# Layer 3's last element: the final check in the written order behind the last centring, the mean behind the variance, the last normalisation in whole passes

## The chip, the cores and the metric

The kernel runs on one core of a Trainium2 chip. The metric is the device time of one execution in microseconds (us). Before the change it is 1911.26 us, the median of four runs (1908.66 to 1915.75).

## The reference

Sixteen graphs of 1024 nodes with 64 features pass through four layers. Each layer computes something on the graph, adds its input, and normalises every row of 64 to mean 0 and variance 1. The last layer, which the change touches, is an attention with four heads, followed by a second attention over the same adjacency, a leaky ReLU, a normalisation with gamma and beta, and then the residual and the layer's own normalisation:

```python
out_h = _gat_layer(h, mask[None, None], bh[None, :, None, :])
cat = jnp.transpose(out_h, (0, 2, 1, 3)).reshape(B, N, H * D)
z = jax.nn.leaky_relu(cat, negative_slope=0.2)
h2 = jnp.einsum('bnk,dk->bnd', z, Wo)
out2 = _gat_layer(h2, mask[None], bo)
z2 = jax.nn.leaky_relu(out2, negative_slope=0.2)
mu = jnp.mean(z2, axis=-1, keepdims=True)
var = jnp.mean(jnp.square(z2 - mu), axis=-1, keepdims=True)
out = (z2 - mu) * jax.lax.rsqrt(var + LN_EPS) * gamma + beta
...
x = _layernorm(x + out, axis=-1)
```

## The kernel before

Nodes lie on the 128 partitions, eight to each, so that a graph is a tile of 128 x 8 x 64 (a "128x512" instruction goes over a whole graph, a "128x64" one over one eighth of it). The layers run one after the other, and in each the 16 graphs. In layer 3 the work of a graph `b` is cut into bursts; lists named `mids` and `slots` give, by graph and burst, the smaller tasks that go between the attention's units, and `run(plan)` and `run(last)` (L2229) issue all of it. Both stand in a `manual_schedule` for the five engines (L2264): inside it each engine keeps the order in which the program issues its instructions. What stands outside is placed by the scheduler of the framework where it finds room, and it may put it between instructions of the written order.

The last graph, `E` = 15, has nothing behind it that could hide its end. Its tasks at the last burst are, in order (L2149): two of the checks, the second normalisation of graph 14 up to its power (`residual_power`), the sums of the last attention (`add_all`), `last_layer`, `shifted` and later `rows_2` of graph 14, `last_quotient`, and `last_norms` (L1733).

`last_norms` normalises twice. Each time `statistics` (L1717) calls `bn_stats` on VectorE (DVE) for the eight slices of 64, which gives count, mean and squared deviations of even and odd elements. From these it forms on VectorE, in tiles of 128x8, the difference `d` of the two means (L1724), the sum of deviations `var` (L1725), `mean` (L1726), the square of `d` in place (L1727), `var` over 64 plus epsilon (L1728) and the final variance (L1729). GpSimd (POOL) raises it to the power of -0.5 (L1730). The first time, eight instructions over one slice each subtract the mean and multiply with gamma (L1737), and eight more multiply with `rstd`, the power, and add the residual (L1739); beta was added to the residual long before (L2156). The second time, one pass subtracts the mean (L1743, the centring), and two halves are multiplied with `rstd` and stored on the queue of Sync (SP), each as soon as it is there (L1748, L1749).

The kernel is a fast path which is exact only if certain values stay in bounds. `check` (L2246) compares such values with a bound and writes the smallest result into a column of `flags`. The last check, of the attention sums of graph 15, stands behind the written order (L2272): a comparison and a reduction (L2248, L2249), the smallest over all flags (L2274), a transposition by TensorE (PE) so that the 128 partitions come into one row (L2276), the smallest of that row (L2278), and the flag `redo` (L2279). At the kernel's very end every engine loads `redo` into a register (`values_load`, L2289) and branches (L2290): where it is 1, a general path computes everything anew; with these inputs it is 0, and the branch skips it. Sync also asserts that the register lies between 0 and 1. Behind the branch Sync waits for the stores and the engines, and a closing round of drains and semaphores ends the program.

Of the kernel before, what the change touches and what calls it, by code (L numbers as in the profile page):

```python
# [8 lines left out]
F32 = mybir.dt.float32  # L9
# [4 lines left out]
ALU = mybir.AluOpType  # L14
AX = mybir.AxisListType

P = 128
FLT_MAX = 3.4028234e38
LN_EPS = 1e-5
# [8 lines left out]
LEAST_SUM = 1e-25  # L28
# [554 lines left out]
def fast_path(  # L583
# [24 lines left out]
    nc = tc.nc  # L608
    B, N, D = x.shape
    C = N // P  # L610
    H = L3_Wh.shape[0]
# [20 lines left out]
    small = ctx.enter_context(tc.tile_pool(name="small", bufs=4))  # L632
# [11 lines left out]
    def xb(b):  # L644
        return xg[b // GB][:, :, b % GB, :]
# [10 lines left out]
    ident = const.tile([P, P], F32, tag="ident", name="ident")  # L656
# [5 lines left out]
    neg_half = const.tile([P, C], F32, tag="neg_half", name="neg_half")  # L662
# [30 lines left out]
    def two_banks(name):  # L693

        if "s" in rings:
            t = rings["s"].tile([P, 2, HALF], F32, tag="s", name=name)
            return [t[:, i, :] for i in range(2)]
        return [ps_t.tile([P, HALF], F32, tag="t", name=name) for _ in range(2)]

    def one_bank(name):  # L700
        if "s" in rings:
            return two_banks(name)[0]
        return ps_t.tile([P, HALF], F32, tag="t", name=name)

    def bc_last(ap, n):

        return ap.unsqueeze(2).to_broadcast([P, ap.shape[1], n])

    def bc_mid(ap, n):

        return ap.unsqueeze(1).to_broadcast([P, n, ap.shape[1]])
# [614 lines left out]
    sums = const.tile([P, B, H + 1, C], F32, tag="sums", name="sums")  # L1326

    bo, gamma, beta = (const.tile([P, D], F32, tag=k, name=k) for k in ("bo", "gamma", "beta"))
# [294 lines left out]
    def head_out(b):  # L1623
# [93 lines left out]
        def statistics(src):  # L1717
            st = small.tile([P, C, 6], F32, tag="bn2", name="bn2", bufs=2)
            for c in range(C):
                nc.vector.bn_stats(st[:, c, :], src[:, c, :])  # L1720
            d, var, mean, rstd = (
                small.tile([P, C], F32, tag=f"last_{k}", name=f"last_{k}", bufs=2) for k in ("d", "var", "mean", "rstd")
            )
            nc.vector.tensor_tensor(d, st[:, :, 1], st[:, :, 4], ALU.subtract)  # L1724
            nc.vector.tensor_tensor(var, st[:, :, 2], st[:, :, 5], ALU.add)  # L1725
            nc.vector.scalar_tensor_tensor(mean, d, 0.5, st[:, :, 4], ALU.mult, ALU.add)  # L1726
            nc.vector.scalar_tensor_tensor(d, d, 0.25, d, ALU.mult, ALU.mult)  # L1727
            nc.vector.tensor_scalar(var, var, 1.0 / D, LN_EPS, ALU.mult, ALU.add)  # L1728
            nc.vector.tensor_tensor(var, var, d, ALU.add)  # L1729
            nc.gpsimd.tensor_tensor(rstd, var, neg_half, ALU.pow)  # L1730
            return mean, rstd

        def last_norms():  # L1733
            v, m = held["v"], held["m"]
            mean, rstd = statistics(v)
            for c in range(C):
                nc.vector.scalar_tensor_tensor(m[:, c, :], v[:, c, :], mean[:, c : c + 1], gamma, ALU.subtract, ALU.mult)  # L1737
            for c in range(C):
                nc.vector.scalar_tensor_tensor(  # L1739
                    v[:, c, :], m[:, c, :], rstd[:, c : c + 1], xb(b)[:, c, :], ALU.mult, ALU.add  # L1740
                )
            mean, rstd = statistics(v)
            nc.vector.tensor_tensor(m, v, bc_last(mean, D), ALU.subtract)  # L1743
            res = ep.tile([P, C, D], F32, tag="m", name="res", bufs=4)
            o = out[b].rearrange("(p c) d -> p c d", c=C)
            for h in range(2):
                part = slice(h * CH, (h + 1) * CH)
                nc.vector.tensor_tensor(res[:, part], m[:, part], bc_last(rstd[:, part], D), ALU.mult)  # L1748
                nc.sync.dma_start(o[:, part], res[:, part])  # L1749
# [61 lines left out]
        def residual_power():  # L1811
            residual_sum()
            held["n2"] = statistics(held["m"])
# [129 lines left out]
    with tc.tile_pool(name="ps_g", bufs=1, space=bass.MemoryType.PSUM, reuse_waits="tile") as ps_g, tc.tile_pool(  # L1943
        name="ps_u", bufs=2, space=bass.MemoryType.PSUM, reuse_waits="tile"
# [167 lines left out]
    E = B - 1  # L2112
# [69 lines left out]
    with tc.tile_pool(name="ps_g", bufs=1, space=bass.MemoryType.PSUM, reuse_waits="tile") as ps_g, tc.tile_pool(  # L2182
        name="ps_p", bufs=1, space=bass.MemoryType.PSUM, reuse_waits="tile"
# [32 lines left out]
    for b in range(B):  # L2216
        units = work[b][0][0] + work[b][1][0]
        outer = outs[b - 1][1][0] if b else []
        for j in range(BURSTS):
            n = (2, 2, 3, 5)[j - 4] if b >= E - 1 and j >= 4 else 5 if j < 4 else 3  # L2220
            burst, units = units[:n], units[n:]
            m = 5 - n
# [6 lines left out]
    def run(plan):  # L2229
        for b, j, burst in plan:  # L2230
            catch_up()
            made = [(unit, unit[0]()) for unit in burst]
            tasks(mids, b, j)
            while roots:
                roots.pop(0)()
            drain()
            made = [(product, mask(e)) for (_, mask, product), e in made]
            waiting.extend(lambda product=product, e=e: product(e) for product, e in made)
            if (b, j, burst) == plan[-1]:
                drain()  # L2240
            tasks(slots, b, j)

    flags = small.tile([P, 11], F32, tag="flags", name="flags", bufs=1)
    nc.vector.memset(flags, 1.0)

    def check(i, ap, op, bound):  # L2246
        t = small.tile([P, B * (H + 1) * C], F32, tag="ok", name="ok", bufs=1)[:, : ap.shape[1]]
        nc.vector.tensor_scalar(t, ap, bound, None, op)  # L2248
        nc.vector.tensor_reduce(flags[:, i : i + 1], t, AX.X, ALU.min)  # L2249

    known = []
# [8 lines left out]
    def look(some):  # L2260
        for one in some:
            check(known.index(one), *one)

    with tc.manual_schedule(engines=in_order | {mybir.EngineType.SP}):  # L2264
        run(plan)
        run(last)

    check(len(known), sums[:, E, H, :], ALU.is_ge, LEAST_SUM)  # L2272
    least = small.tile([P, 1], F32, tag="least", name="least")
    nc.vector.tensor_reduce(least, flags, AX.X, ALU.min)  # L2274
    pl = one_bank("pl")
    nc.tensor.transpose(pl[:1, :P], least, ident)  # L2276
    least1 = small.tile([1, 1], F32, tag="least1", name="least1")
    nc.vector.tensor_reduce(least1, pl[:1, :P], AX.X, ALU.min)  # L2278
    nc.vector.tensor_scalar(redo, least1, -1.0, 1.0, ALU.mult, ALU.add)  # L2279


def kernel(tc, *args):


    nc = tc.nc
    with tc.tile_pool(name="flag", bufs=1) as fp:
        redo = fp.tile([1, 1], I32, tag="redo", name="redo")
        fast_path(tc, redo, *args)
        again = nc.values_load(redo[0:1, 0:1], min_val=0, max_val=1)  # L2289
        with tc.If(again == 1):  # L2290
            general_path(tc, *args)
# [32 lines left out]
```

## Time and profile before

| what | value |
|---|---|
| median of four runs | 1911.26 us |
| the profiled execution | 1917.18 us, of which the span is 1915.4 us |
| mean granted TensorE clock | 0.987 |
| TensorE busy | 1863.6 us (97%) |
| VectorE busy | 1746.7 us (91%) |
| ScalarE busy | 1322.7 us (69%) |
| GpSimd busy | 102.0 us (5%) |
| VectorE busy, 1904.00 to 1907.70 | 3.60 of 3.70 us |
| VectorE busy, 1907.70 to 1910.00 | 0.77 of 2.30 us |
| GpSimd busy, 1907.70 to 1910.00 | 1.93 us |

The page gives busy time by engine over the whole span, in which the last fifteen microseconds count for less than one per cent. They are read from the timeline (one row for an instruction or a run of like ones, with its start from the beginning of the span, its time, line, operation, output and inputs, and in brackets the idle time of its engine before it and what ended it) and from the view of one line, which also has what a sequencer does by itself: loads of registers, branches and waits. These are not counted as busy time. Durations of neighbours can overlap: an instruction may start before the one ahead of it has ended, if it doesn't read its result.

### The profile page before, as it was taken

What the parts mean: (1) busy time and instruction counts of PE and PEld (TensorE: products, weight loads), DVE (VectorE), ACT (ScalarE), POOL (GpSimd) and SP (SyncE); (2) the same over time, 40 slices, a digit from 0 to 9 for tenths busy, and PEclk for the clock granted to TensorE, in tenths of its full rate; (3) what the DMA queues carried; (4) which work ended last, traced back from release to release, by engine and by line L of the source; (5) the groups of instructions that cost most, each with busy time, mean ns of one, the idle gap of its engine ahead of it and who ended that gap; (6) DMA issues with size and microseconds to landing.
All of it is one profiled execution on the core that took longest, in us unless ns stands there. A gap on an engine that the chain in (4) does not pass through costs nothing. (4 is left out here: it accounts for less than half of the span.)

```text
span 1915.4 us, 25738 instructions
## 1 busy us (share of the span) xinstructions
PE 1863.6 (97%) x9505; PEld 768.0 (40%) x9505; DVE 1746.7 (91%) x2913; ACT 1322.7 (69%) x2336; POOL 102.0 (5%) x93
## 2 busy tenths in 40 slices
PE   8999989999999999999999999999999999999996
PEld 4344337874433333333333333333333333333332
DVE  6899998899999988899998998999989899899996
ACT  3556567867888677676777667767667766776754
POOL 0000000001121000000000000000000000000001
PEclk8999989999999999999999999999999999999998
DMA  7000000002232300000010000100001000010000
GB/s 184 1 1 1 1 1 1 1 1 17 23 26 25 89 12 19 17 12 18 12 29 18 12 18 12 27 20 12 18 13 29 18 12 18 13 29 18 12 23 13
DMA packets 60308, 39.56 MB, mean 21 GB/s; under 512 B 51855, under 2 KB 52176, under 8 KB 60174
## 3 DMA queue, kind: packets, MB, share of 16 engines
q1 hardware_dynamic: 43534, 33.64, 6.7%
q0 software_dynamic: 14560, 3.67, 2.5%
q8 instruction: 76, 1.25, 0.3%
q10 hardware_dynamic: 2080, 0.52, 0.1%
q14 instruction: 58, 0.48, 0.1%
HBM read 29.45 MB, written 4.70 MB: 18 GB/s over the span
## 5 line engine op out<-in xcount | busy, mean ns | idle before, releaser
L1469 ACT ACTIVATE e<-s,shift 128x1024 f32<-128x1024 f32 x512 | 539.1, 1123 | 239.4 <-PE s L1465 239.4
L1473 DVE TENSOR_TENSOR e<-e,aT 128x1024 f32<-128x1024 f32 x512 | 597.8, 1218 | 3.1 <-ACT e L1469 2.9
L1465 PE MATMUL s<-hT 64*128 64x512 f32 x2048 | 489.1, 602 | 1.6 <-ACT zT L1512 1.2
L1480 PE MATMUL y<-e,vals 128*64 128x512 f32 x2048 | 483.4, 599 | 1.8 <-DVE e L1473 0.9
L1465 PEld LDWEIGHTS s<-hT 64*128 64x128 f32 x2048 | 183.9, 185 | 286.7 <-issue 143.5
L1480 PEld LDWEIGHTS y<-e,vals 128*64 128x64 f32 x2048 | 135.2, 136 | 269.0 <-issue 197.5
L1053 DVE SCALAR_TENSOR_TENSOR e<-G_l,q,aT 128x1024 f32<-128x1024 f32 x150 | 185.9, 1276 | 1.2 <-ACT G_l L1012 0.6
L1649 DVE TENSOR_TENSOR e<-e,aT 128x1024 f32<-128x1024 f32 x128 | 156.4, 1225 | 13.1 <-ACT e L1636 3.1
L1065 PE MATMUL y_l<-e,vals_l 128*64 128x512 f32 x608 | 146.2, 608 | 2.5 <-DVE e L1053 2.3
L1641 DVE SCALAR_TENSOR_TENSOR junk<-e,aN 128x1024 bf16<-128x1024 f32 x120 | 146.0, 1217 | 0.0
L1636 ACT ACTIVATE e<-s,shift 128x1024 f32<-128x1024 f32 x128 | 138.7, 1114 | 4.0 <-PE s L1631 3.9
L1631 PE MATMUL s<-h2T 64*128 64x512 f32 x512 | 127.5, 598 | 0.0
L1657 PE MATMUL y<-e,h2v 128*64 128x512 f32 x512 | 125.6, 592 | 0.0
L1408 POOL PARTITION_ALL_REDUCE gtop<-top x48 | 54.6, 1137 | 1214.7 <-DVE top L1406 1047.1
L2031 PE MATMUL po<-hi,aR 128*128 128x512 f32 x256 | 102.9, 403 | 10.9 <-ACT hi L1935 7.1
L2031 PE MATMUL po<-lo,aR 128*128 128x512 f32 x256 | 101.1, 396 | 0.3 <-DVE lo L1936 0.3
L793 ACT ACTIVATE x<-m,bn_shift,bn_rstd 128x64 f32<-128x64 f32 x216 | 74.6, 429 | 18.5 <-DVE bn_shift L784 18.5
L1631 PEld LDWEIGHTS s<-h2T 64*128 64x128 f32 x512 | 51.8, 189 | 60.1 <-issue 37.6
L1512 ACT COPY zT<-poT 64x512 f32<-64x512 f32 x124 | 72.0, 581 | 1.1
L1065 PEld LDWEIGHTS y_l<-e,vals_l 128*64 128x64 f32 x608 | 38.4, 136 | 76.0 <-issue 61.0
L1487 ACT COPY yT<-y 128x512 f32<-128x512 f32 x64 | 38.5, 601 | 43.5 <-PE y L1480 42.2
L1657 PEld LDWEIGHTS y<-e,h2v 128*64 128x64 f32 x512 | 36.6, 137 | 73.5 <-issue 59.5
(305 smaller groups left out, 2163.1 us busy)
## 6 DMA issues: line engine op xcount, KB each, us to landing
r<-inverse SPq DMA_DIRECT2D x62, 256.0 KB
adj<-in_adj_dram SPq DMA_DIRECT2D x16, 512.0 KB
out_dram<-res SPq DMA_DIRECT2D x15, 256.0 KB
x<-in_x_dram SPq DMA_DIRECT2D x14, 256.0 KB
m<-x POOLq DMA_DIRECT2D x14, 256.0 KB, 5.1
rows<-yT SPq DMA_DIRECT2D x62, 4.0 KB
x<-in_x_dram ACTq DMA_DIRECT2D x2, 256.0 KB
sums<-rows SPq DMA_DIRECT2D x31, 8.0 KB
```

Source lines behind the costliest of these rows:

```text
L1053: nc.vector.scalar_tensor_tensor(e, of_pair(b - b % 2, b % 2), pq[b - b % 2][1][:, k, b % 2 : b % 2 + 1], aT[:, k, :], ALU.max, ALU.mult,)
L1065: nc.tensor.matmul(held["y"][h * D : (h + 1) * D, :], vals[b][:, k, :], e[:, h * HALF : (h + 1) * HALF], start=(k == 0), stop=(k == C - 1),)
L1465: nc.tensor.matmul(s[:, i, :], hT[rows, k * P : (k + 1) * P], hT[rows, cols], start=True, stop=True)
L1469: nc.scalar.activation(e, s, AF.Exp, bias=shifts[b, n])
L1473: nc.vector.tensor_tensor(e, e, bc_mid(aT[:, k, h * HALF : (h + 1) * HALF], 2), ALU.mult)
L1480: nc.tensor.matmul(held[h][i * D : (i + 1) * D, :], vals[b][:, k, :], e[:, i, :], start=(k == 0), stop=(k == C - 1),)
L1631: nc.tensor.matmul(s[:, i, :], hT[rows, (i + k // CH) % 2, k % CH * P : (k % CH + 1) * P], hT[rows, 0, :], start=True, stop=True,)
L1636: nc.scalar.activation(e, s, AF.Exp, bias=shifts[b])
L1641: nc.vector.scalar_tensor_tensor(junk.rearrange("p c q -> p (c q)").bitcast(BF16), e.rearrange("p i q -> p (i q)"), 1.0, aN[:, k, :], ALU. ...
L1649: nc.vector.tensor_tensor(e, e, aT[:, k, :].rearrange("p (i q) -> p i q", i=2), ALU.mult)
L1657: nc.tensor.matmul(held["o"][h * D : (h + 1) * D, :], vals["out", b][:, k, :], e[:, h, :], start=(k == 0), stop=(k == C - 1),)
L2031: nc.tensor.matmul(po.rearrange("p q k f -> p (q k f)"), aR[:, k, ic * P : (ic + 1) * P], e[:, k].rearrange("p q k f -> p (q k f)"), start ...
```

## The change

Three things. In `statistics`, the mean goes behind the power, and the square of `d` gets a tile of its own (`last_square`), since `mean` still reads `d`. In `last_norms`, the first normalisation is four passes over the whole tile (subtract the mean, times gamma, times the power, plus the residual) where it was sixteen instructions over slices. And the last check moves, unchanged in itself, from behind the written order into it: `last_check` is called between the centring and the product with the last power. `statistics` also serves graph 14 (`residual_power`), so that the new order holds there too.

```diff
             nc.vector.tensor_tensor(d, st[:, :, 1], st[:, :, 4], ALU.subtract)
             nc.vector.tensor_tensor(var, st[:, :, 2], st[:, :, 5], ALU.add)
+            nc.vector.tensor_scalar(var, var, 1.0 / D, LN_EPS, ALU.mult, ALU.add)
+            square = small.tile([P, C], F32, tag="last_square", name="last_square", bufs=2)
+            nc.vector.scalar_tensor_tensor(square, d, 0.25, d, ALU.mult, ALU.mult)
+            nc.vector.tensor_tensor(var, var, square, ALU.add)
+            nc.gpsimd.tensor_tensor(rstd, var, neg_half, ALU.pow)
             nc.vector.scalar_tensor_tensor(mean, d, 0.5, st[:, :, 4], ALU.mult, ALU.add)
-            nc.vector.scalar_tensor_tensor(d, d, 0.25, d, ALU.mult, ALU.mult)
-            nc.vector.tensor_scalar(var, var, 1.0 / D, LN_EPS, ALU.mult, ALU.add)
-            nc.vector.tensor_tensor(var, var, d, ALU.add)
-            nc.gpsimd.tensor_tensor(rstd, var, neg_half, ALU.pow)
             return mean, rstd
...
         def last_norms():
             v, m = held["v"], held["m"]
             mean, rstd = statistics(v)
-            for c in range(C):
-                nc.vector.scalar_tensor_tensor(m[:, c, :], v[:, c, :], mean[:, c : c + 1], gamma, ALU.subtract, ALU.mult)
-            for c in range(C):
-                nc.vector.scalar_tensor_tensor(
-                    v[:, c, :], m[:, c, :], rstd[:, c : c + 1], xb(b)[:, c, :], ALU.mult, ALU.add
-                )
+            nc.vector.tensor_tensor(m, v, bc_last(mean, D), ALU.subtract)
+            nc.vector.tensor_tensor(m, m, bc_mid(gamma, C), ALU.mult)
+            nc.vector.tensor_tensor(m, m, bc_last(rstd, D), ALU.mult)
+            nc.vector.tensor_tensor(v, m, xb(b), ALU.add)
             mean, rstd = statistics(v)
             nc.vector.tensor_tensor(m, v, bc_last(mean, D), ALU.subtract)
+            last_check()
             res = ep.tile([P, C, D], F32, tag="m", name="res", bufs=4)
...
+    def last_check():
+        check(len(known), sums[:, E, H, :], ALU.is_ge, LEAST_SUM)
+        least = small.tile([P, 1], F32, tag="least", name="least")
+        nc.vector.tensor_reduce(least, flags, AX.X, ALU.min)
+        pl = one_bank("pl")
+        nc.tensor.transpose(pl[:1, :P], least, ident)
+        least1 = small.tile([1, 1], F32, tag="least1", name="least1")
+        nc.vector.tensor_reduce(least1, pl[:1, :P], AX.X, ALU.min)
+        nc.vector.tensor_scalar(redo, least1, -1.0, 1.0, ALU.mult, ALU.add)
+
     with tc.manual_schedule(engines=in_order | {mybir.EngineType.SP}):
         run(plan)
         run(last)
```

The same lines, from `check(len(known), ...)` to `redo`, are taken out behind `run(last)`.

More of the change, by code (lines that the diff above doesn't have):

```diff
@@ L2266, in fast_path @@
         run(last)
[L2272 to L2279, printed above, removed]
 def kernel(tc, *args):
```

## The prediction

> **What bounds the kernel.** I began with the page. The tensor engine is busy 97% of the span, so for nearly all of it only work taken off TensorE could save time. The chain that ended last shows where that stops:
>
> ```profile
> span 1915.4 us, 25738 instructions
> ...
> POOL last_rstd L1730 0%; DVE res L1748 0%; DVEq L2289 0%; POOLq L2289 0%
> ```
>
> The end hangs on GpSimd's last power (L1730), VectorE's last product (L1748) and the loads of the flag (L2289). The diff touches only this end: TensorE's last matmul of the layer ends near 1898.5, and from there to 1915.4 VectorE works through the last element alone. So I went to the timeline of VectorE (start, us, instruction, and in brackets the idle time before it):
>
> ```profile
> 1901.02 0.17 DVE L1724 TENSOR_TENSOR last_d<-bn 128x8 f32<-128x8 f32 x1
> 1901.11 0.17 DVE L1725 TENSOR_TENSOR last_var<-bn 128x8 f32<-128x8 f32 x1
> 1901.23 0.17 DVE L1726 SCALAR_TENSOR_TENSOR last_mean<-last_d,bn 128x8 f32<-128x8 f32 x1
> 1901.61 0.28 DVE L2278 TENSOR_REDUCE least<-pl 1x1 f32<-1x128 f32 x1 [0.20 <-PE pl L2276]
> 1901.81 0.14 DVE L1727 SCALAR_TENSOR_TENSOR last_d<-last_d 128x8 f32<-128x8 f32 x1
> 1901.89 0.15 DVE L1728 TENSOR_SCALAR last_var<-last_var 128x8 f32<-128x8 f32 x1
> 1901.96 0.13 DVE L2279 TENSOR_SCALAR redo<-least 1x1 int32<-1x1 f32 x1
> 1902.08 0.17 DVE L1729 TENSOR_TENSOR last_var<-last_var,last_d 128x8 f32<-128x8 f32 x1
> 1902.16 1.65 DVE L1737 SCALAR_TENSOR_TENSOR m<-v,last_mean,gamma 128x64 f32<-128x64 f32 x8
> 1904.00 1.66 DVE L1739 SCALAR_TENSOR_TENSOR v<-m,last_rstd,x 128x64 f32<-128x64 f32 x8 [0.19 <-POOL last_rstd L1730]
> 1905.57 1.11 DVE L1720 BATCH_NORM_STATS2 bn<-v 128x6 f32<-128x64 f32 x8
> ...
> 1907.41 0.17 DVE L1729 TENSOR_TENSOR last_var<-last_var,last_d 128x8 f32<-128x8 f32 x1
> 1907.49 0.68 DVE L1743 TENSOR_TENSOR m<-v,last_mean 128x512 f32<-128x512 f32 x1
> 1909.70 0.76 DVE L1748 TENSOR_TENSOR res<-m,last_rstd 128x256 f32<-128x256 f32 x2 [1.53 <-POOL last_rstd L1730]
> ```
>
> Two things are to be seen. The final check is not at the end: its steps (L2278, L2279) are threaded through the first of these statistics. And VectorE waits 1.53 us for the second power, which is the room that the change wants to fill. GpSimd's own timeline gives the two powers:
>
> ```profile
> 1902.32 1.64 POOL L1730 TENSOR_TENSOR last_rstd<-last_var,neg_half 128x8 f32<-128x8 f32 x1 [4.15 <-DVE last_var L1729]
> 1907.74 1.93 POOL L1730 TENSOR_TENSOR last_rstd<-last_var,neg_half 128x8 f32<-128x8 f32 x1 [3.78 <-DVE last_var L1729]
> ```
>
> Last, who reads the flag, by line L2289 (each engine's own load, its ns, when it starts):
>
> ```profile
> L2289 SPq TENSOR_LOAD <-redo x1: 667/667/667, 1902.1 to 1902.1; - x1
> L2289 ACTq TENSOR_LOAD <-redo x1: 716/716/716, 1902.1 to 1902.1; - x1
> L2289 PEldq TENSOR_LOAD <-redo x1: 738/738/738, 1902.1 to 1902.1; - x1
> ...
> L2289 DVEq TENSOR_LOAD <-redo x1: 540/540/540, 1909.7 to 1909.7; - x1
> ```
>
> Sync, ScalarE and TensorE load the flag the moment it is written, at 1902.1, eight microseconds ahead of the last stores. After the change the flag is written beside the last product, and these loads move there.
>
> **The sum, up to the last product.** I set t = 0 at L1724 of the first statistics (1901.02); the last product stands at 1909.70, that is 8.68.
>
> Check taken out of the first statistics. From L1724 to L1729 it takes 1902.08 - 1901.02 = 1.06; the second statistics, with no check between, takes 1907.41 - 1906.71 = 0.70. Gain 0.36. The check's other steps (L2248, L2249, L2274) cost nothing today: each starts within 0.12 of the step before it and the next dependent step starts 0.03 to 0.04 behind its own input all the same; without them nothing gets earlier.
>
> Mean behind variance. The rows show 0.09 between independent small steps and 0.03 from the end of one to the start of one that reads it. By these: d at 0.00, var 0.09, scale and eps 0.29, square 0.38, sum 0.58, ending at 0.75, against 0.70 + 0.17 = 0.87. The power starts 0.12 earlier, twice; the mean now ends at 0.83 and its subtraction starts at 0.86 instead of 0.79, which only the power's cover sees. The same gain on the element before (its power, 1896.47 to 1898.16) is worth nothing: VectorE then waits for ScalarE's copy until 1898.03, and the shift that reads the power starts at 1898.64 behind other work.
>
> Whole passes. A 128x512 pass took 0.68 to 0.69 (L1804, L1805, L1743), and one starts 0.04 behind the other. Beside the power lie two of them, 0.86 to 1.54 and 1.58 to 2.26. The power ends at 0.75 + 0.08 + 1.64 = 2.47, so the third runs 2.51 to 3.19 and the fourth 3.23 to 3.92; the statistics follow at 3.96. Before, they started at 1905.57 - 1901.02 = 4.55. Gain 0.59, made of 0.36 check, 0.12 order, and 0.11 for two passes in place of eight slices (the first slice of bn_stats no longer overlaps the last slice's end, which is in it).
>
> Second statistics and check. They need 1.14 for bn_stats (1905.57 to 1906.71), then 0.75 to the variance. The power takes until 2.47 at 1.64, or 2.85 at the 1.93 and later start (0.17) of the second power. VectorE centres 0.86 to 1.54, then the check in order: compare 1.46 to 1.58 (it starts before the pass ends, as L2249 does today), reduce 1.61 to 1.76, reduce 1.79 to 1.94; the transposition costs 0.56 between them (L2274 ends 1901.05, L2278 starts 1901.61), with the clock at 0.5 in both; reduce 2.50 to 2.78, flag 2.81 to 2.94. The product starts behind the flag's start, at 2.89. Before it was 1909.70 - 1906.71 = 2.99. Gain 0.10: the check has the time of the power and is a little longer than it, so it, not the power, is late next. If that cover failed wholly (the check after the power) it would cost its own 1.4.
>
> Up to the last product: 0.59 + 0.10, **0.69 earlier**.
>
> **The sum, behind the last product.** The end comes by the stores: product at +0, first store +0.46, second +0.90 (1910.6), its landing lets Sync's last waits go at 1913.1, +3.4, and then the closing waits run to 1915.4. What is moved is the flag's readers. (a) Sync. In the trace its load stands in its queue ahead of the two stores, and they are queued behind it; with its register step and assertion it holds Sync from 1902.1 for 0.98 us. If that order stays, it starts at +0.08, the first store at +1.12 instead of +0.46: **0.66 later**, and both stores, and the end, with it. If the load goes behind the stores, it lies under their landing and costs nothing. The trace can't show the order after; the nearest row is the load's place today, so I take 0.66 and keep 0. (b) TensorE: load 0.74, then its branch 3.48 (line L2290), so it is through at about +4.5; the last drain of Sync is at 1914.5, +4.8. Hidden, by 0.3 with (a) at zero and 1.0 with (a). (c) ScalarE, GpSimd and VectorE resume 2.5 to 2.9 after their branches: +3.2 to +3.7, hidden too.
>
> Sum: -0.69 + 0.66 = -0.03 us. On the profiled execution (1917.18, span 1915.4 plus 1.78 around it) that makes 1917.15. That execution lies 5.9 over the median of the runs, 1911.26; the end's steps are the same in both, so I put the difference on the median: **1911.2**.
>
> [...]
>
> [...]
>
> **Rivals.** (1) Sync's load goes behind the stores: -0.69, 1910.6. For it: GpSimd's load and VectorE's came only at their last work, so loads don't always go first; against it: Sync's did. (2) Slower: whole passes and the power hold each other up, which the slices did not. The place is the first two passes and the centring. The price from the rows: the power beside L1743 against the one beside L1737, 1.93 - 1.64 + 0.09 later start = 0.38, on the first statistics alone (in the second, 2.85 is under the check's 2.89): -0.03 + 0.38, 1911.6. At the far end, with passes that are held for as long as the power runs, the first starts at 2.50 instead of 0.86, bn_stats at 5.39 instead of 3.96 (+1.4), and in the second the centring and the check behind it +1.6: 1914.2. It decides from 0.03 us of hindrance on. Against it stands the pace of L1737. (3) The gain is there and TensorE's branch takes it: only if (a) is zero and the branch grows by over 0.3. VectorE's gap, beside the stores, was 2.9 against GpSimd's 2.6 alone; by the same ratio the branch would take 3.9 and cost 0.1: 1910.7. (4) The change doesn't do what it says, the check not beside the power: then the check's 1.4 stands open, less the 0.10, and 1912.6. Against it: the check is now in the order written by hand.
>
> **Numbers.** Chances: my forecast 0.42, (1) 0.28, (2) 0.20, (3) 0.05, (4) 0.05. All cases lie between 1910.6 and 1914.2. The four runs before spread from -2.6 to +4.5 about their median, without any change, so the range is wider than the cases on the low side: 1908.0 to 1915.0. By more than 0.3% (5.7 us, about what a measurement of this kernel can tell from no change) none of the cases gets away; what I leave to both sides is the scatter of medians and what another layout of the same work might do: faster 0.04, same 0.91, slower 0.05.
>
> **What would show it.** After the change the steps from L1724 to the sum of the variance (L1729 today) should take 0.58 in both statistics; four passes near 0.69, the third starting within 0.05 of the power's end; the check behind the centring with the flag ending near 2.9 from L1724; almost no idle time of VectorE between flag and last product. Sync's load ahead of the stores, and the first store over a microsecond behind the last product's start, show (a); otherwise (1). The power over 1.8 us beside the passes, or a pass over 0.75, shows (2). I am wrong if the closing waits are set by an engine's branch, or if anything before 1896 moves.

## The result and the profile after

The changed kernel takes 1913.61 us (median of 32 runs, 1911.64 to 1918.32) against 1911.35 us for the kernel before (52 runs). The ratio is 1.0013, with a 95% interval of 1.0008 to 1.0018: slower by about 2.5 us (1.5 to 3.4). The profiled execution took 1914.02 us, its span 1912.2 us. That span is shorter than the 1915.4 us of before, since the layers ahead of the end happened to run faster in it; spans of single executions differ by more than the change, so I compare the end by itself. Below, the *end piece* is the time from L1724 of the first of the two last statistics to the end of the span: 1915.39 - 1901.02 = 14.37 us before, 1912.23 - 1895.95 = 16.28 us after, 1.9 us more.

VectorE's timeline of the changed kernel (start, us, instruction; in brackets the idle time):

```profile
1895.95 0.17 DVE L1724 TENSOR_TENSOR last_d<-bn 128x8 f32<-128x8 f32 x1
...
1896.51 0.17 DVE L1729 TENSOR_TENSOR last_var<-last_var,last_square 128x8 f32<-128x8 f32 x1
...
1896.76 1.64 POOL L1730 TENSOR_TENSOR last_rstd<-last_var,neg_half 128x8 f32<-128x8 f32 x1 [3.80 <-DVE last_mean L1731]
1896.80 0.71 DVE L1737 TENSOR_TENSOR m<-v,last_mean 128x512 f32<-128x512 f32 x1
1897.54 0.69 DVE L1738 TENSOR_TENSOR m<-m,gamma 128x512 f32<-128x512 f32 x1
1898.43 0.69 DVE L1739 TENSOR_TENSOR m<-m,last_rstd 128x512 f32<-128x512 f32 x1 [0.20 <-POOL last_rstd L1730]
1899.16 0.69 DVE L1740 TENSOR_TENSOR v<-m,x 128x512 f32<-128x512 f32 x1
1899.88 1.11 DVE L1720 BATCH_NORM_STATS2 bn<-v 128x6 f32<-128x64 f32 x8
1901.03 0.17 DVE L1724 TENSOR_TENSOR last_d<-bn 128x8 f32<-128x8 f32 x1
...
1901.87 0.69 DVE L1742 TENSOR_TENSOR m<-v,last_mean 128x512 f32<-128x512 f32 x1
1901.93 2.13 POOL L1730 TENSOR_TENSOR last_rstd<-last_var,neg_half 128x8 f32<-128x8 f32 x1 [3.53 <-DVE last_mean L1731]
...
1903.92 0.14 DVE L2272 TENSOR_SCALAR redo<-least 1x1 int32<-1x1 f32 x1
1904.09 0.76 DVE L1748 TENSOR_TENSOR res<-m,last_rstd 128x256 f32<-128x256 f32 x2
```

Up to the last product the change does most of what it should: 8.15 us from L1724 to L1748, 8.68 before. The loss lies behind it: from the last product to the end it is 1912.2 - 1904.1 = 8.1 us, and 1915.4 - 1909.7 = 5.7 us before. Once that product is done (0.76 us) no engine computes there. The stretch is read from the lines of the flag's loads, of the branch and of the program's last line (number of events, ns, first and last start):

```profile
L2286 ACTq TENSOR_LOAD <-redo x1: 484/484/484, 1904.1 to 1904.1; - x1
L2286 POOLq TENSOR_LOAD <-redo x1: 492/492/492, 1904.1 to 1904.1; - x1
L2286 PEldq TENSOR_LOAD <-redo x1: 491/491/491, 1904.1 to 1904.1; - x1
L2286 DVEq TENSOR_LOAD <-redo x1: 546/546/546, 1904.1 to 1904.1; - x1
L2286 SPq TENSOR_LOAD <-redo x1: 484/484/484, 1905.4 to 1905.4; - x1
```

```profile
L2287 SPq EVENT_SEMAPHORE  x8: 17/17/17, 1906.5 to 1908.8; - x8
L2287 ACTq COMPARE_BRANCH  x1: 54/54/54, 1904.6 to 1904.6; - x1
...
L2287 PEldq COMPARE_BRANCH  x1: 3524/3524/3524, 1904.7 to 1904.7; - x1
...
L2287 ACTq EVENT_SEMAPHORE  x1: 17/17/17, 1908.6 to 1908.6; - x1
```

```profile
L2316 SPq DRAIN  x3: 7/7/7, 1910.0 to 1910.4; - x3
L2316 PEldq DRAIN  x2: 8/8/8, 1908.4 to 1910.4; - x2
L2316 ACTq DRAIN  x2: 8/64/121, 1908.7 to 1911.9; - x2
L2316 DVEq DRAIN  x2: 10/14/17, 1908.7 to 1910.4; - x2
```

The branch in the kernel before:

```profile
L2290 SPq EVENT_SEMAPHORE  x8: 17/17/17, 1911.2 to 1913.2; - x8
L2290 ACTq COMPARE_BRANCH  x1: 54/54/54, 1902.9 to 1902.9; - x1
...
L2290 ACTq EVENT_SEMAPHORE  x1: 17/17/17, 1905.5 to 1905.5; - x1
```

Four engines load the flag in the same instant and branch at 1904.6 to 1904.7. ScalarE needs until 1908.6 for it, 4 us; before it branched at 1902.9 and was through at 1905.5. Two things end late. The last of Sync's eight waits, the stores among them, is let go at 1908.8, 4.7 us behind the last product (before: 1913.2, 3.5). And in the closing round ScalarE's last drain comes at 1911.9, where the other engines' come at 1910.4 to 1910.7. In the same view of before nobody is that far behind:

```profile
L2319 SPq DRAIN  x3: 7/7/7, 1914.5 to 1914.8; - x3
L2319 ACTq DRAIN  x2: 8/65/122, 1905.6 to 1915.1; - x2
L2319 PEldq DRAIN  x2: 8/8/8, 1906.7 to 1915.1; - x2
L2319 DVEq DRAIN  x2: 10/14/17, 1913.4 to 1914.8; - x2
```

What lies there instead of work is seen in the DMA queues from the last product to the end (queue, kind: packets, MB, share of the 16 engines). The kernel before:

```profile
q1 hardware_dynamic: 288, 0.26, 14.2%
q14 instruction: 4, 0.03, 2.1%
```

and the changed one:

```profile
q1 hardware_dynamic: 288, 0.26, 13.0%
q14 instruction: 7, 0.06, 2.6%
q8 instruction: 2, 0.03, 1.7%
```

The first line in each is the stores. What the other queues carry, of the kind "instruction", I read as code; it comes in pieces of 8 KB (16 KB on q8, where a piece starts 1.0 to 1.2 us behind TensorE's branch in both kernels): four pieces before, nine after. In the trace the first four of the changed kernel start 1.5 to 1.8 us behind the last product, as many as engines had branched by then, just where the stores' data move (1.3 to 2.3). Single packets of the stores then take up to 0.54 us where most take 0.05, and the last of them ends at +4.1 (before: +2.9). Sync had issued the two stores equally early in both, 0.45 and 0.89 us behind the start of the product.

The trace also has when each of the 16 parts of a store has landed. Of the second store's, 14 had landed by +2.7 in the kernel before, and the other two came at +3.3 and +3.4; two pieces of code had started beside the stores (+1.4 to +2.4). In the changed kernel four pieces had started there, and four parts were late, at +3.9 to +4.6.

### The profile page after: what moved, and what is told of

The parts are those of the page before. It is cut to its first block, busy times and chain, and to the rows that moved or that the text cites. A ratio compares the mean times of both kernels' runs of the same rounds, so it can differ in the third digit from the quotient of the medians.

```text
span 1912.2 us, 25727 instructions
## 1 busy us (share of the span) xinstructions
PE 1858.8 (97%) x9505; PEld 762.1 (40%) x9505; DVE 1746.8 (91%) x2901; ACT 1322.3 (69%) x2336; POOL 102.6 (5%) x93
## 3 DMA queue, kind: packets, MB, share of 16 engines
q0 software_dynamic: 14560, 3.67, 2.2%
q8 instruction: 76, 1.25, 0.3%
## 4 chain that ended last, share of the span: by engine, by line
PE 66%; DVE 26%; ACT 4%; issue 2%; DMA 1%; POOL 0%; SPq 0%; DVEq 0%; ACTq 0%
PE y L1480 19%; PE s L1465 19%; DVE e L1473 5%; PE s L1631 5%; PE y L1657 4%; PE po L2031 4%; PE y_l L1065 4%; DVE e L1053 4%; DVE e_hi L1053 3%; DVE e_lo L1053 3%; PE u_l L1077 2%; DVE e L1649 2%; DVE junk L1641 1%; PE ph2T L1582 1%; PE phT L1439 1%
```

## The experiments

**Theory F (fetch), a supposition from the traces of before and after.** Writing the flag late makes all engines branch at once at the very end (in the changed kernel four at 1904.6 to 1904.7). The pieces of code that start behind the branches (+1.5 to +1.8 us) delay the stores, and the closing round waits for a second set of pieces (from +4.9). **Rival P.** The new work on VectorE, or the layout that shifts with it, costs the time elsewhere.

The table puts all runs together. Columns: flag written, relative to the last product; L1724 to the last product; last product to the end; their sum, the end piece; Sync's wait for the second store let go, behind the last product (all from the traces, one execution each, us); measured ratio to the kernel before and its 95% interval. The kernels were timed in three sets, in which the kernel before took 1911.53 us (e1, e2, flag early and late), 1918.12 (flag mid, e4, e5) and 1911.35 (e6, e7); times compare only within a set, and the times expected below are meant for a kernel before of 1911.3. The ratios resolve about 0.1% (1.9 us); the traces of the end resolve 0.1 us, and from one execution of the same kernel to the next the stretch behind the last product differed by 0.1 (the two kernels that ran twice).

| kernel | flag | to product | behind it | end piece | store | ratio |
|---|---|---|---|---|---|---|
| before | -7.6 | 8.68 | 5.69 | 14.37 | 3.4 | |
| changed | 0.0 | 8.15 | 8.14 | 16.28 | 4.6 | 1.0013 [1.0008, 1.0018] |
| e1 check outside | -7.3 | 8.25 | 5.49 | 13.74 | 3.2 | 0.9997 [0.9988, 1.0006] |
| e7 the same again | -7.3 | 8.25 | 5.58 | 13.83 | 3.3 | 0.9998 [0.9986, 1.0009] |
| e2 check only | 0.0 | 8.32 | 7.75 | 16.07 | 4.4 | 1.0008 [0.9999, 1.0017] |
| e3 flag early | -5.6 | 8.22 | 5.93 | 14.15 | 3.6 | 0.9999 [0.9990, 1.0008] |
| e3 flag mid | -2.2 | 8.15 | 5.80 | 13.95 | 3.5 | 0.9993 [0.9981, 1.0005] |
| e7 flag mid again | -2.2 | 8.14 | 5.76 | 13.90 | 3.5 | 0.9993 [0.9980, 1.0006] |
| e3 flag late | -1.5 | 8.14 | 6.23 | 14.36 | 3.2 | 1.0004 [0.9995, 1.0013] |
| e4 before, no branch | (-7.6) | 8.68 | 3.68 | 12.36 | 2.7 | 0.9990 [0.9976, 1.0003] |
| e4 changed, no branch | (0.0) | 8.15 | 3.67 | 11.82 | 2.7 | 0.9979 [0.9966, 0.9993] |
| e5 ScalarE's code moved | 0.0 | 8.15 | 7.57 | 15.72 | 4.3 | 0.9994 [0.9982, 1.0007] |
| e6 both moved, changed | 0.0 | 8.14 | 6.76 | 14.90 | 4.5 | 0.9995 [0.9985, 1.0004] |
| e6 both moved, e1 | -7.3 | 8.25 | 5.75 | 14.01 | 3.5 | 0.9992 [0.9982, 1.0002] |

**e1: the check outside again.** `last_check()` is taken out of `last_norms`, and its eight lines stand behind `run(last)` as before.

> The changed kernel, but the last check stands behind the written order again, as before; the new order of the statistics and the whole passes stay. Theory F (the late flag: all engines branch together at the end, and their fetches of code meet the last stores and the closing round): the flag is written early again, the end behind the last product is 5.7 us long as in the kernel before (8.1 in the changed one), and what the passes and the order save remains, 0.2 to 0.4 us: 1911.0, that is 0.02% under the kernel before. Rival P (the new VectorE work of the end, or its shifted layout, costs the time somewhere else): the kernel stays at 1913 to 1914, 0.1% over the kernel before, and the end stays at 8.1.

The end behind the last product is 5.5 us, the time 1910.81 against 1911.53: F's case. The interval, below that of the changed kernel, excludes a loss of 0.13%; a gain over the kernel before is not resolved. The last product, from VectorE's timeline, waits for the power again:

```profile
1903.52 0.76 DVE L1747 TENSOR_TENSOR res<-m,last_rstd 128x256 f32<-128x256 f32 x2 [1.53 <-POOL last_rstd L1730]
```

**e2: the check alone.** The reverse of e1: the kernel before, with only this part of the diff:

```diff
             nc.vector.tensor_tensor(m, v, bc_last(mean, D), ALU.subtract)
+            last_check()
             res = ep.tile([P, C, D], F32, tag="m", name="res", bufs=4)
```

> The kernel before, with the last check alone moved into the written order behind the last centring; statistics and first normalisation as before. Theory F: the 0.36 us of the check leave the first statistics, the end behind the last product grows from 5.7 to about 8.1 us: 1913.3, 0.1% over the kernel before. Rival P: no loss, 1911.0.

The end behind the last product is 7.75 us, with the old statistics and slices, 0.4 less than expected: the check's place alone makes 2.1 of the 2.45 us that the end grew by. The measured ratio, 1.0008, has 1 just inside its interval. Here it is not ScalarE that comes last but TensorE, whose last semaphore of the closing round starts at 1910.9, the others' at 1909.9 to 1910.0 (program's last line):

```profile
L2321 ACTq EVENT_SEMAPHORE  x2: 17/17/17, 1909.3 to 1910.0; - x2
L2321 DVEq EVENT_SEMAPHORE  x2: 21/21/21, 1909.3 to 1910.0; - x2
L2321 PEldq EVENT_SEMAPHORE  x2: 51/51/51, 1909.3 to 1910.9; - x2
```

**e3: only the flag's place in time.** The check is cut into five steps, of which four go where VectorE has room; the fifth, the 1x1 instruction that writes `redo`, stands at one of three places (mid is behind the last step of the second statistics). The cut is drawn together from the three kernels; each has the one call that its word behind # names:

```diff
             mean, rstd = statistics(v, last_least)
             nc.vector.tensor_tensor(m, v, bc_last(mean, D), ALU.subtract)
             nc.vector.tensor_tensor(m, m, bc_mid(gamma, C), ALU.mult)
+            last_row()
+            last_redo()                                              # early
...
-            mean, rstd = statistics(v)
+            mean, rstd = statistics(v, None, last_redo)              # mid
             nc.vector.tensor_tensor(m, v, bc_last(mean, D), ALU.subtract)
+            last_redo()                                              # late
```

> The changed kernel with the check cut into its steps and these put, in the written order, where VectorE waits anyway or starts nothing late: comparison and reduction in the last quotient, the smallest flag behind the first bn_stats, the row and the flag behind the product with gamma, beside the first power. Theory F: the flag is written about 5.5 us ahead of the last product; the three branches are through before the stores, the end behind the last product is 5.7 us, and the row and flag cost 0.2 to 0.3 in the first power's time: 0.2 to 0.5 us under the kernel before, 1910.9. Rival P: 1913 to 1914.

> The same as the kernel with the early flag, except that one instruction, the one that writes the 1x1 flag, stands behind the last centring. VectorE does the same work in both. Theory F: this instruction alone brings the loss back: the end behind the last product is about 8 us, and the kernel is 2.0 to 2.5 us slower than the one with the early flag. Rival P: the two kernels take the same time within 0.3 us.

> As the kernels with the early and the late flag, with the flag written behind the second statistics, about 2.1 us ahead of the last product. Theory F, as a matter of the place in time: TensorE's branch takes 3.5 us from its load on and would be through 2.3 us behind the last product, well ahead of the closing round, and most fetches lie ahead of the stores: the end behind the last product is 5.7 to 6.3 us and the time is within 0.6 us of the early flag. [...]

Mid came as F has it (5.8), and early nearly so (5.9 for 5.7); P's loss of about 0.1% lies outside both intervals. Late did not come as expected: 6.2 in place of 8, 0.3 over early instead of 2. The reason is in VectorE's timeline: the 1x1 instruction reads nothing of the centring (1901.77 to 1902.46) and started 0.08 us before its end, so that the flag was there 1.5 us ahead of the product:

```profile
1902.38 0.13 DVE L2292 TENSOR_SCALAR redo<-least 1x1 int32<-1x1 f32 x1
1903.99 0.76 DVE L1755 TENSOR_TENSOR res<-m,last_rstd 128x256 f32<-128x256 f32 x2 [1.48 <-POOL last_rstd L1734]
```

So it is a point between mid and the changed kernel, and a telling one: the stores are not late (3.2), three of the four first pieces of code were over at +1.2, before the stores' data moved, and still TensorE's last drain comes at 1910.0, the other engines' at 1908.9 to 1909.2:

```profile
L2336 ACTq DRAIN  x2: 8/65/122, 1906.2 to 1909.2; - x2
L2336 PEldq DRAIN  x2: 8/8/8, 1906.7 to 1910.0; - x2
L2336 DVEq DRAIN  x2: 10/14/17, 1907.6 to 1908.9; - x2
```

That separates the two halves of the loss. It also gives a length for TensorE, from the flag's end to its late step in the closing round: 7.5 us here, 7.7 in e2, 7.6 in e5. From these three lengths I estimate that a flag that is not to hold up the closing round has to be written that much ahead of it, in this kernel some 2 us before the last product.

**e4: no branch.** Loads, branch and general path are gone from both kernels:

```diff
         fast_path(tc, redo, *args)
-        again = nc.values_load(redo[0:1, 0:1], min_val=0, max_val=1)
-        with tc.If(again == 1):
-            general_path(tc, *args)
```

> The changed kernel without the loads of the flag, the branch and the general path behind it: the flag is written and nobody reads it. Left out is thus the second computation for inputs out of bounds. Theory F: nothing is fetched from a far place; the first store lands 1.9 us behind its issue (3.8 in the changed kernel), ScalarE's last drain comes with the others, the end behind the last product is at most 5.7 us, and the kernel is at least 2.4 us faster than the changed one: 1911.2 or less. Rival P: the time stays at 1913 to 1914.

> The kernel before without the loads of the flag, the branch and the general path; the same is left out as in its twin of the changed kernel. Theory F: here the branches were nearly hidden, so it gains less than 0.7 us; the changed kernel without the branch is then 0.4 to 0.7 us faster than this one, which is what VectorE saved up to the last product. Rival P: the changed one stays 2 us slower than this one.

Both need 3.7 us behind the last product, and the changed one now has the shorter end piece by 0.54. It is 0.21% (0.07 to 0.34%) faster than the kernel before, and its end piece is 4.5 us shorter than the changed kernel's, where at least 2.4 was expected. The queues from the last product to the end hold the stores and nothing else:

```profile
q1 hardware_dynamic: 288, 0.26, 20.4%
```

For the kernel before I had expected a gain under 0.7 us: by the trace it is 2.0 (its timing, 0.9990, has 1 inside the interval). The branch was less hidden there than I thought, with VectorE's own branch still beside the stores (their wait 3.4 against 2.7). From that wait to the end it takes 2.3 us with the branch and 1.0 without; Sync, which had 22 semaphore events behind its branch, has 11 there.

**e5 and e6: the code moved.** At the end of the general path, which is skipped, stand instructions that are never executed; e5 has the first two lines, e6 all (the two tiles that they write are made ahead of them, not shown):

```diff
+    for _ in range(64):
+        nc.scalar.copy(idle, headroom)
+    for _ in range(48):
+        nc.tensor.transpose(idle_t[:, :P], ident, ident)
```

> The changed kernel with 64 more ScalarE copies at the end of the general path, which the branch skips: no instruction more is executed, only ScalarE's code behind the branch lies 64 places further on. Theory F, its half on the closing round (ScalarE runs into code that is not there yet, between its last semaphore and its last drain): the edge of the fetched piece lies elsewhere, ScalarE's last drain comes within 0.3 us of the others (1.6 later in the changed kernel), and the time falls by 1.2 us. If that wait has another cause, neither drain nor time moves.

> The changed kernel with 64 more ScalarE copies and 48 more TensorE transpositions at the end of the general path, which the branch skips, so that the code behind the branch lies further on for both. With ScalarE's code alone moved, its late drain was gone, but TensorE came last, 1.5 us behind the others. Theory F, with the second piece of code as the cause of the late closing: now neither is late, the closing round passes without a wait, and the end behind the last product is 6.3 to 6.8 us (8.1 in the changed kernel, 7.6 with ScalarE's code alone moved); the last store still lands at 4.2 to 4.6, for the first fetches meet it as before. If TensorE was late for another reason, the end stays at 7.5 or more.

> The kernel with the new statistics and passes and the check behind the written order, with the same additions to the skipped general path. Theory F: with an early flag the second piece is there long before the closing round, so little is left to gain: the end behind the last product goes from 5.5 to between 5.1 and 5.5 us, the time to 0.6 to 1.0 us under the kernel before. If the moved code mattered by itself, it would gain as much here as in the changed kernel, over 1 us.

In e5 ScalarE's last drain comes with the others, as expected, but the end is only 0.6 us shorter, not 1.2: TensorE's last semaphore was right behind and is now the last one. The timing of e5 is not clear of the kernel before.

```profile
L2321 ACTq DRAIN  x2: 8/8/8, 1916.8 to 1918.9; - x2
L2321 DVEq DRAIN  x2: 10/14/17, 1917.3 to 1918.9; - x2
...
L2321 DVEq EVENT_SEMAPHORE  x2: 21/21/21, 1918.8 to 1919.4; - x2
L2321 PEldq EVENT_SEMAPHORE  x2: 51/51/51, 1918.8 to 1920.5; - x2
```

In e6, with both moved, none is late, and the end behind the last product falls to 6.8 us, 1.4 less than in the changed kernel:

```profile
L2324 ACTq DRAIN  x2: 8/8/8, 1907.0 to 1910.0; - x2
L2324 DVEq DRAIN  x2: 10/14/17, 1907.8 to 1910.0; - x2
...
L2324 DVEq EVENT_SEMAPHORE  x2: 21/21/21, 1909.9 to 1910.5; - x2
L2324 PEldq EVENT_SEMAPHORE  x2: 51/51/51, 1909.9 to 1910.5; - x2
```

The interval, 0.9985 to 1.0004, lies below that of the changed kernel, though not one executed instruction of the computation differs. The store's wait stays late (4.5), as expected: four pieces of code start beside the stores here too. With the check outside, the same additions gain nothing (5.75 for an expected 5.1 to 5.5; 5.5 and 5.6 without them): from the second store's wait to the end it takes about 2.3 us there as in e1, but that wait was let go 0.2 to 0.3 later in that execution.

**e7.** e1 and the mid flag once more.

> The kernel with the new statistics and passes and the check behind the written order, once more, since its first interval reached from 0.12% under to 0.06% over the kernel before. From its trace 0.6 us, 0.03%, under the kernel before; theory F puts it at 1910.7 if the kernel before is at 1911.3, rival P at 1913 or more.

> The kernel with the flag about 2.2 us ahead of the last product, once more, beside the others. From its trace (5.8 us behind the last product) 0.4 us under the kernel before; theory F says the same as for the early flag, rival P 1913 or more.

Both ends came out as the first time, within 0.1 us. Their medians, 1911.61 and 1911.02 against 1911.35, leave open whether they beat the kernel before; by the traces the shortest is e1, by 0.6 us. No version here is faster than the kernel before clear of the scatter of the timings, but for the changed kernel without the branch.

## Why the prediction was wrong, step by step

- **First statistics and whole passes**, predicted 0.59 earlier: 5.08 us from L1724 to L1724, 5.69 before, 0.61. Right in each term: the last step of the variance at 0.56 (0.58), the third pass 0.03 behind the power, passes of 0.69 to 0.71, bn_stats at 3.93 (3.96).
- **Second statistics**, predicted 0.10 earlier: 3.07 us, 0.07 later than before (2.99). The term that was mis-sized is the duration of the power. It took 2.13 us, not 1.64 to 1.93, and ended at 1904.06, as late as the check's flag. In e1, without a check there, the product waits for it just as long (3.06). The row of 1.93 gave the hint and I used it as a bound: in both traces, and to 0.01 in the twelve others, the power ends 1.50 us after the centring beside it (1908.17 to 1909.67; 1902.56 to 1904.06). With the mean behind the variance the centring ends 0.80 after the variance's last step has ended, before 0.59. So this reordering delayed the second power, where I counted a gain of 0.12. e2 has the old order and the check behind the centring: its second statistics take 2.99, as before. So the check's steps cost nothing up to the last product, and the order costs the 0.07.
- **Rival (2)** was therefore half there: the price is about 0.2 us and in the second statistics, not the first, where the power that starts ahead of the pass took 1.64. Where the pass started first (1907.49 against 1907.74 before, 1901.87 against 1901.93 in the changed kernel), the power ended 1.50 behind the pass; where the power started first (1896.76), the pass 0.04 behind it took 0.71 us, beside 0.69 for the next one. No run shows why. Nor does any show passes held for as long as the power runs, the far end of 1914.2.
- **(a) Sync**, taken at 0.66 out of 0 to 0.66: zero. Sync's load stood behind the stores (1905.4, the stores at 1904.55 and 1904.98), as rival (1) had it. The order of before was no guide.
- **(b) and (c), "hidden too"**: this is the step that failed, the loss put at nothing. My times for the branches, taken one by one, were TensorE through at +4.5 and the others at +3.2 to +3.7. They were +4.2 and +4.5 to +4.6. I asked only whether each would be through before Sync's last drain at +4.8 (a misreading: the row has three drains, the first at 1914.5, the last at 1914.8, +5.1). Two consequences were left out. Pieces of code start beside the stores, and these were let go 1.2 us later (second store, by trace: 2.7 with no code beside it, 3.2 to 3.6 with one to three pieces, 4.3 to 4.6 with four). And an engine that is through its branch can still come late in the closing round: in the changed kernel a second set of pieces starts at +4.9 to +5.4, ScalarE's last drain comes 1.5 us behind TensorE's and VectorE's (in e2 and e5 TensorE's last semaphore is late, by 0.9 and 1.1), and from the second store's wait to the end it takes 1.25 us longer than before; with the code moved (e6) it takes as long as before, 2.3. Together 1.20 + 1.25 = 2.45, the whole growth from 5.69 to 8.14.
- **The gaps behind the branch.** In every trace with a branch four of the five engines go on 2.6 to 4.3 us behind it, Sync 0.2 us behind its own. The sum has nothing for all of them branching at once.
- **The size.** The sum was -0.69 + 0.66; by the traces it was -0.54 + 2.45 = +1.9, and the timings say 1.5 to 3.4. That everything stays within 0.3% was right, and that the measured time lies among my cases (1910.6 to 1914.2) was luck: none of them had this cause. Rival (3), TensorE's branch, came nearest, but its branch was through earlier than I had it, not later. What came true is a sign that I had named for being wrong: the closing waits are set by the engines' branches. That the end's steps carry over from one execution to another holds to 0.1 us in the two kernels that ran twice.

Shown by runs: that the flag's place makes the loss (e1, e2, e3, e4), and that the place of skipped code makes about half of it (1.4 of 2.45 us in e6, by the traces). Not shown is how the pieces of code make the stores late; what the landings show is that the two go together. In 13 of the 14 traces as many of the second store's 16 parts land over 0.2 us behind the rest as pieces of code start between +1.4 and +2.4 (none in e4, one in flag late, two to four in the others); flag mid again has three pieces and two late parts. Nor is it shown what it is about the code's place that e5 and e6 changed; the edge of a fetched piece was my supposition.

## What to carry to other kernels

A flag that all engines branch on should be written well before the last stores: in this kernel the end behind the last product was 8.1 us with the flag beside that product, and 5.8 with the flag 2.2 us ahead of it. Idle time of the computing engine near the end was not free for work whose result the sequencers wait for: in e2 it cost 2.1 us behind the last product. When a step is moved, follow its readers on every engine to the end of the program, and look at what moves in the DMA queues behind them.

## What the runs showed of the hardware

- TensorE's branch took 3.4 to 4.1 us where one or two other engines branched with it, and 3.5 to 4.2 where all four did; ScalarE went on 2.6 to 3.1 us behind its branch, and 2.6 to 4.0. The ranges overlap: how many engines branch together does not settle it.
- Skipped code had a price by its place (e5, e6): 64 instructions that never run took away the 1.5 us by which ScalarE's last drain was late, and 48 more for TensorE another 0.8 us from the end.
- Without the branch the end behind the last product was 3.7 us (e4), in the best kernel with it (e1) 5.5: the never-taken path cost 1.8 us there.
- The power on GpSimd took 1.64 us where it started ahead of the pass beside it, and ended 1.50 us behind the whole pass that had started before it, in all 14 traces, whether its record was 1.93 or 2.13 us long (old and new order).
- Of the second store's 16 parts as many landed late as pieces of code started beside it, in 13 of the 14 traces: none without a branch, two in the kernel before, four in the changed one.
